# Layer 1 of a two-layer graph network: the running weighted sum, the projections, bias and gate accumulated in PSUM

## The chip, the core and the metric

The kernel runs on one core of one Trainium2 chip. The metric is the device time of one execution in microseconds (us), the median of several runs. TensorE (PE in the profile), VectorE (DVE), ScalarE (ACT) and GpSimd (POOL) each take their instructions in program order and wait for each other through semaphores; the SyncE queue (SP) issues plain DMAs, and GpSimd issues all indirect DMAs (gathers and scatters).

## What is computed

A graph of 3327 nodes with 512 features each and an adjacency matrix `adj` with few ones per row (at most 128 rows of nodes have many). Layer 0 is a four-head graph attention; its result is added to `x` and normalised. This `x` goes into layer 1, which the change is about. Cut to what matters, with `adj` as both of its adjacencies:

```
type_sum = adj @ x
attn_a = sigmoid(concat(type_sum, x) @ Wa.T + ba)        # one number per node
attn_b = sigmoid(concat(type_sum, x) @ Wb.T + bb)
h = x @ W_sa
scores = s_left[:, None] + s_right[None, :]              # two dot products of h with a_sa
e = where(adj != 0, exp(-leaky_relu(scores, 0.01)), 0)
attn = e / (sum(e, axis=1) + 1e-5)
x_a = attn @ h
x_b = adj @ (x @ W_gcnb) + b_gcnb
x = layernorm(x + sigmoid(attn_a * x_a + attn_b * x_b))
```

## The kernel before

Everything is float32. The nodes are sorted by degree and cut into 26 tiles of 128 nodes, in two groups of 12 and 14. `CAPS[j]` says how many neighbours tile j needs at most (14 down to 4); a neighbour is a slot, and a slot of a tile is one gather of 128 rows of 520 floats (266 KB) by GpSimd (`indirect`, L615) into one of 42 slots of a ring in SBUF. The first tile of each group (`T0`) has one slot more, the "stair", for the few nodes with more neighbours than `CAPS`. Over layer 1 this makes 228 gathers: 226 slots and 2 stairs.

Layer 1 uses linearity: instead of summing rows of h and of `x @ W_gcnb`, it sums rows of x, weighted and plain, and projects the two sums. For one tile j:

- `own_score`, `weights_a`, `weights_b` (L1019 to L1065): VectorE and ScalarE make the weights `e[:, s]` of the slots, already multiplied by the gate `attn_a`, from columns that travel with the rows; `gates[j][:, 1:2]` is the gate `attn_b`. VectorE's L1032 is the first that reads a tile's gathered rows, L1039 is ScalarE's exp, L1062 the last scaling of the weights.
- `scaled_first` (L1067): ScalarE starts the weighted sum `sw`, an SBUF tile, with the node's own row (L1070). For a `T0` tile it also scales the stair and TensorE spreads it (`stair_sum`, L1075).
- `weighted` (L1077), in two parts: one VectorE instruction per slot adds row times weight onto `sw` (L1085, a scalar_tensor_tensor over 128x512).
- `plain_sum` (L1089): TensorE adds the rows up in PSUM, transposed already, four instructions a row (L1098).
- `turn`, `to_sbuf`, `project` (L1103 to L1118): TensorE transposes `sw` (L1107), ScalarE copies both sums from PSUM into SBUF (L1112; half 1 the plain, half 0 the weighted one), TensorE multiplies each with its weight matrix into PSUM tiles `po0` (one buffer) and `po1` (two buffers). A float32 instruction of the program runs as two rows of the trace there: the four steps of a `project` are eight rows "po L1118".
- L1147 to L1149: VectorE adds the bias to `po1` (L1147), multiplies by the gate and adds `po0` (L1148), ScalarE takes the tanh in SBUF (L1149). Later VectorE adds it to the residual (L1171), takes the statistics (L692), and every few tiles the normalisation runs (L701 to L708 on VectorE, L1161 on ScalarE) and GpSimd scatters the rows out (L146).

The order is written out by hand, as a software pipeline over 26 + 3 steps. In step i tile `j` = order[i] is summed, `j1` = order[i+1] gets its weights, `jp` = order[i-1] is projected, `jpp` = order[i-2] is finished. Within a step the order per engine is: TensorE `turn(jp)`, `plain_sum(j)`, `project(jp, 1)`, `project(jp, 0)`, then the small products for `j1` if it is a `T0` tile; VectorE `weighted(j, 0)`, bias and gate of `jpp`, `weights_a(j1)`, `weighted(j, 1)`, residual of `jpp`, `weights_b(j1)`, statistics; ScalarE the plain copy of `jp`, the weighted copy of `jp`, tanh of `jpp`, exp and gate of `j1`, normalisation, `scaled_first(j1)`. GpSimd issues gathers as soon as the ring has free slots, and the scatters of finished rows only when no gather is left.

Of the kernel before, what the change touches and what calls it, by code (L numbers as in the profile page):

```python
# [8 lines left out]
F32 = mybir.dt.float32  # L9
AF = mybir.ActivationFunctionType  # L10
ALU = mybir.AluOpType
# [3 lines left out]
P = 128  # L15
# [63 lines left out]
def sparse_pass(  # L79
# [39 lines left out]
    nc = tc.nc  # L119
    N, F = out.shape  # L120
    NP = x.shape[0]
    H, FO = a_self.shape
# [61 lines left out]
    def row1(j):  # L184
        g, i = place(j)
        return x1[g][:, i, :]
# [827 lines left out]
        order += long[:1] + short[:1]  # L1014
        short, long = short[1:], long[1:]
    order += last
    ew, gates, sums, plain, proj, zs, stair_sum = {}, {}, {}, {}, {}, {}, {}

    def own_score(j):  # L1019
        ew[j] = m1.tile([P, S + 1], F32, tag="e", name=f"e{j}", bufs=3)  # L1020
# [2 lines left out]
    def weights_a(j):  # L1023

        c = slots(j)
        e = ew[j]
        gate = gates[j] = m1.tile([P, 12], F32, tag="gate", name=f"gate{j}", bufs=5)
        if j in T0:
            small = ps1.tile([P, B * H], F32, tag="small", name=f"to_nodes1_{j}")
            cols = to_nodes(m1, small, f"l1_{j}", stair[j][:, F : F + 3])  # L1030
        for s0, n, g, _ in got[j]:
            nc.vector.tensor_scalar(e[:, s0 : s0 + n], g[:, :n, F], row1(j)[:, F + 3 : F + 4], None, ALU.add)  # L1032
# [12 lines left out]
        if j in T0:  # L1045
            nc.vector.tensor_reduce(
                gate[:, 4 + 2 * parts : 6 + 2 * parts], cols[:, :, 1:3].rearrange("p b i -> p i b"), AX.X, ALU.add
            )
            parts += 1
        nc.vector.tensor_add(gate[:, 0:2], gate[:, 4:6], row1(j)[:, F + 4 : F + 6])  # L1050
        for i in range(1, parts):
            nc.vector.tensor_add(gate[:, 0:2], gate[:, 0:2], gate[:, 4 + 2 * i : 6 + 2 * i])

        nc.scalar.activation(gate[:, 0:2], gate[:, 0:2], AF.Tanh, scale=0.5)

    def weights_b(j):
# [5 lines left out]
        nc.vector.tensor_scalar(e[:, :c], e[:, :c], gate[:, 2:3], gate[:, 0:1], ALU.mult, ALU.mult)  # L1062
        if j in T0:
            small = ps1.tile([P, B * H], F32, tag="small", name=f"to_rows1_{j}")
            ws2[j] = to_rows(m1, small, f"l1_{j}", e[:, C0 + 1 :].rearrange("p (b o) -> p b o", o=1))  # L1065

    def scaled_first(j):  # L1067

        sw = sums[j] = m1.tile([P, F], F32, tag="sw", name=f"sw{j}")
        nc.scalar.activation(sw, row1(j)[:, 0:F], AF.Copy, scale=ew[j][:, 0:1])  # L1070
        if j in T0:
            scaled = m1.tile([P, F], F32, tag="scaled", name=f"scaled{j}", bufs=1)
            nc.scalar.activation(scaled, stair[j][:, 0:F], AF.Copy, scale=ws2[j])
            stair_sum[j] = ps1.tile([P, F], F32, tag="stair", name=f"stair_sum{j}")
            nc.tensor.matmul(stair_sum[j], to_node, scaled, start=True, stop=True)  # L1075

    def weighted(j, part):  # L1077

        e, sw = ew[j], sums[j]
        cut = 2 + (CAPS[j] * 5 + 7) // 8  # L1080
        for s0, n, g, _ in got[j]:
            for i in range(n):
                s = s0 + i
                if (s < cut) == (part == 0):
                    nc.vector.scalar_tensor_tensor(sw, g[:, i, 0:F], e[:, s : s + 1], sw, ALU.mult, ALU.add)  # L1085
        if part == 1 and j in T0:
            nc.vector.tensor_add(sw, stair_sum[j], sw)

    def plain_sum(j):  # L1089

# [20 lines left out]
        sT = zs[j, half] = m1.tile([P, KT, P], F32, tag=f"sT{half}", name=f"sT{half}_{j}")  # L1111
        nc.scalar.copy(sT, (turned, plain)[half][j])  # L1112

    def project(j, half):
        sT, wt = zs[j, half], (wsa, wg)[half]
        po = proj[j, half] = ps1.tile([P, F], F32, tag=f"po{half}", name=f"po{half}_{j}", bufs=1 + half)
        for k in range(KT):
            nc.tensor.matmul(po, sT[:, k, :], wt[:, k, :], start=(k == 0), stop=(k == KT - 1))  # L1118

    ends = {3, 7, 11, 15, 19, 22, 24, 25}  # L1120
    norm = Norm(m1, "n1", ends)
# [9 lines left out]
    for i in range(NT + 3):  # L1131
        j, j1, jp, jpp = at_(i), at_(i + 1), at_(i - 1), at_(i - 2)
        if i > 0 and jp is not None:
            free(jp)
        gather()
        if j1 is not None:
            own_score(j1)
        if jp is not None:
            to_sbuf(jp, 1)
            turn(jp)  # L1140
            to_sbuf(jp, 0)
        if j is not None:
            plain_sum(j)
            weighted(j, 0)
        if jpp is not None:
            za = zs[jpp] = m1.tile([P, F], F32, tag="za", name=f"za{jpp}", bufs=3)
            nc.vector.tensor_add(za, bias_g, proj[jpp, 1])  # L1147
            nc.vector.scalar_tensor_tensor(za, za, gates[jpp][:, 1:2], proj[jpp, 0], ALU.mult, ALU.add)  # L1148
            nc.scalar.activation(za, za, AF.Tanh, scale=0.5)  # L1149
        if jp is not None:  # L1150
            project(jp, 1)
            project(jp, 0)
        if j1 is not None:
            weights_a(j1)
        if j is not None:
            weighted(j, 1)
        if ready:
            k0, scale, shift = ready
            for k in range(k0, i - 2):
                z = row1(order[k])[:, 0:F]  # L1160
                nc.scalar.activation(  # L1161
                    z, z, AF.Identity, scale=scale[:, k - k0 : k - k0 + 1], bias=shift[:, k - k0 : k - k0 + 1]
                )
                outs.append((own(order[k]), z))
            ready = None
        while outs and not waiting:
            scatter("out", out, *outs.pop(0), N - 1)
        if jpp is not None:
            za = zs[jpp]
            zs[jpp] = row1(jpp)[:, 0:F]  # L1170
            nc.vector.scalar_tensor_tensor(zs[jpp], za, 0.5, zs[jpp], ALU.mult, ALU.add)  # L1171
        if j1 is not None:
            weights_b(j1)
            scaled_first(j1)
        if jpp is not None:
            ready = norm.add(i - 2, zs[jpp])

# [451 lines left out]
```

## Time and profile before

| | us |
|---|---|
| time before, median of 3 runs (1057.76 to 1071.53) | 1068.92 |
| profiled execution, its own time | 897.77 |
| its span, from the first to the last instruction | 895.8 |
| TensorE busy / VectorE busy / GpSimd busy / ScalarE busy | 745.3 / 693.3 / 595.2 / 272.0 |
| first and last issue of the 228 gathers of layer 1 | 530.94 / 842.26 |
| end of TensorE's last instruction of layer 1 | 879.8 |
| mean granted TensorE clock | 0.908 |

The span is one execution recorded by the profiler; 1.97 us lie around it. The median of the runs is 171.15 us above the profiled execution's own time. The profile page doesn't say where these are. Times of instructions below are microseconds from the start of the span. A group line gives the count, the busy time, the mean duration of one in ns, and the idle time of the engine before it with what ended it. A line of the timeline gives the start, the length, the engine and the count of the merged instructions.

### The profile page before, as it was taken

What the parts mean: (1) busy time and instruction counts of PE and PEld (TensorE: products, weight loads), DVE (VectorE), ACT (ScalarE), POOL (GpSimd) and SP (SyncE); (2) the same over time, 40 slices, a digit from 0 to 9 for tenths busy, and PEclk for the clock granted to TensorE, in tenths of its full rate; (3) what the DMA queues carried; (4) which work ended last, traced back from release to release, by engine and by line L of the source; (5) the groups of instructions that cost most, each with busy time, mean ns of one, the idle gap of its engine ahead of it and who ended that gap; (6) DMA issues with size and microseconds to landing.
All of it is one profiled execution on the core that took longest, in us unless ns stands there. A gap on an engine that the chain in (4) does not pass through costs nothing. (4 is left out here: it accounts for less than half of the span.)

```text
span 895.8 us, 11378 instructions
## 1 busy us (share of the span) xinstructions
PE 745.3 (83%) x3118; PEld 457.4 (51%) x3118; DVE 693.3 (77%) x2032; ACT 272.0 (30%) x794; POOL 595.2 (66%) x641
## 2 busy tenths in 40 slices
PE   4698997416799978799999957987997999999992
PEld 3477775103445534344444435654764666666551
DVE  4288787896678858769898845957996999998973
ACT  0122221002335525444646512212222222232231
POOL 6711133566577777777777747777777777777772
PEclk9799999556899989889999967999898999999997
DMA  8989999999777878789777637677767777777641
GB/s 330 369 340 403 366 377 345 380 387 399 267 225 227 276 234 263 231 278 329 219 234 228 222 115 203 188 199 201 187 184 196 192 196 195 203 193 199 195 187 74
DMA packets 73352, 224.74 MB, mean 251 GB/s; under 512 B 12736, under 2 KB 16784, under 8 KB 72384
## 3 DMA queue, kind: packets, MB, share of 16 engines
q0 software_dynamic: 46368, 153.69, 56.9%
q1 hardware_dynamic: 24256, 68.13, 19.9%
q10 hardware_dynamic: 2656, 2.10, 0.7%
q8 instruction: 27, 0.44, 0.2%
q14 instruction: 45, 0.37, 0.1%
HBM read 203.02 MB, written 31.51 MB: 262 GB/s over the span
## 5 line engine op out<-in xcount | busy, mean ns | idle before, releaser
L615 POOL DMA_INDIRECT ring<-table,srt x464 | 475.7, 1025 | 162.1 <-issue 56.2
L803 PE MATMUL acc<-ring,ident 128*128 128x512 f32 x504 | 239.4, 619 | 18.9 <-DVE ring L802 12.9
L1085 DVE SCALAR_TENSOR_TENSOR sw<-ring,e,sw 128x512 f32<-128x512 f32 x226 | 169.8, 751 | 10.7 <-ACT sw L1070 4.2
L803 PEld LDWEIGHTS acc<-ring,ident 128*128 128x128 f32 x504 | 94.4, 196 | 130.3 <-issue 74.3
L371 PE MATMUL pf<-w,xc 128*128 128x260 f32 x416 | 102.9, 410 | 13.1 <-DVE w L311 13.1
L1098 PE MATMUL acc<-ident,ring 128*128 128x128 f32 x904 | 108.6, 280 | 6.2 <-DMA ring<-table,srt 6.1
L797 DVE TENSOR_TENSOR ring<-ring,w 128x512 f32<-128x512 f32 x176 | 111.8, 693 | 0.5
L1098 PEld LDWEIGHTS acc<-ident,ring 128*128 128x128 f32 x904 | 103.6, 145 | 8.1 <-DMA ring<-table,srt 8.1
L1118 PE MATMUL po<-wsa,sT 128*128 128x512 f32 x208 | 95.4, 602 | 4.6 <-DVE za L1148 2.3
L371 PEld LDWEIGHTS pf<-w,xc 128*128 128x128 f32 x416 | 84.1, 205 | 29.3 <-DVE w L311 13.8
L1118 PE MATMUL po<-wg,sT 128*128 128x512 f32 x208 | 93.6, 593 | 0.0
L795 ACT ACTIVATE ring<-ring,w 128x128 f32<-128x128 f32 x304 | 91.5, 390 | 0.0
L383 POOL DMA_DIRECT2D table<-row x26 | 14.2, 549 | 85.2 <-ACT st L380 82.6
L1118 PEld LDWEIGHTS po<-wsa,sT 128*128 128x128 f32 x208 | 39.7, 193 | 56.6 <-issue 56.1
L1118 PEld LDWEIGHTS po<-wg,sT 128*128 128x128 f32 x208 | 37.5, 190 | 37.3 <-issue 37.3
L1149 ACT ACTIVATE za<-za 128x512 f32<-128x512 f32 x26 | 16.4, 630 | 127.7 <-DVE za L1148 127.7
L402 PE MATMUL pc<-at,pow 128*32 128x512 bf16 (+1 forms) x182 | 23.3, 413 | 35.3 <-DMA at<-in_adjB 25.4
L762 ACT ACTIVATE w<-w 128x40 f32<-128x40 f32 (+10 forms) x26 | 6.2, 237 | 127.5 <-DVE w L761 127.5
L375 ACT COPY row<-pf 128x512 f32<-128x512 f32 x26 | 15.2, 586 | 95.4 <-PE pf L371 49.7
L834 PEld LDWEIGHTS pcol<-v,xt 128*128 128x128 f32 x208 | 28.7, 201 | 14.5 <-issue 12.1
L828 ACT COPY xt<-x1t 128x512 f32<-128x512 f32 x26 | 15.2, 584 | 62.9 <-PE x1t L822 62.9
L402 PEld LDWEIGHTS <-pow 128*32 128x32 bf16 x182 | 7.3, 97 | 47.9 <-issue 44.8
(252 smaller groups left out, 918.4 us busy)
## 6 DMA issues: line engine op xcount, KB each, us to landing
at<-in_adjB SPq DMA_DIRECT2D x78, 512.0 KB, 11.5
ring<-table,srt POOLq DMA_INDIRECT x464, 3.9
table<-row POOLq DMA_DIRECT2D x26, 260.0 KB, 6.1
xc<-in_xB SPq DMA_DIRECT2D x6, 1024.0 KB, 8.4
own<-in_xo SPq DMA_DIRECT2D x1, 3640.0 KB, 46.5
own<-table SPq DMA_DIRECT2D x1, 3640.0 KB, 55.2
at<-in_adjL SPq DMA_DIRECT2D x13, 256.0 KB, 9.9
table<-in_xo SPq DMA_DIRECT2D x1, 3120.0 KB, 27.2
```

Source lines behind the costliest of these rows:

```text
L371: nc.tensor.matmul(pf[:, hh, :HC], xc[:, k, o : o + P], w0[:, k, hh, :], start=(k == 0), stop=(k == KT - 1))
L375: nc.scalar.copy(row[:, 0:F].rearrange("p (h o) -> p h o", h=2), pf[:, :, 0 : F // 2])
L402: nc.tensor.matmul(pc[32 * c : 32 * c + 32, : nt * P], pow2[:, s, :], loaded[i, m], start=(s == 0), stop=(m + 1 not in ms or s == 3),)
L615: return nc.gpsimd.indirect_dma_start(out=out_, out_offset=None, in_=table, in_offset=bass.IndirectOffsetOnAxis(ap=ap, axis=0)).ins
L795: nc.scalar.activation(gv[:, h, :], gv[:, h, :], AF.Copy, scale=w[:, s, h : h + 1])
L797: nc.vector.tensor_tensor(gv, gv, w[:, s, :].rearrange("p (h o) -> p h o", o=1).to_broadcast([P, H, FO]), ALU.mult)
L803: nc.tensor.matmul(acc, ident, row, start=(lean and s == 0), stop=(s == CAPS[j] and j not in T0))
L834: nc.tensor.matmul(pcol, xt1[:, k, :], v1[:, k, :], start=(k == 0), stop=(k == KT - 1))
L1085: nc.vector.scalar_tensor_tensor(sw, g[:, i, 0:F], e[:, s : s + 1], sw, ALU.mult, ALU.add)
L1098: nc.tensor.matmul(pl[:, k, :], row[:, k * P : (k + 1) * P], to_node if steps else ident, start=(i + k == 0), stop=(i == len(rows) - 1 and ...
L1118: nc.tensor.matmul(po, sT[:, k, :], wt[:, k, :], start=(k == 0), stop=(k == KT - 1))
L1149: nc.scalar.activation(za, za, AF.Tanh, scale=0.5)
```

## The change

The weighted sum `so_far` lives in PSUM now: ScalarE writes its first term there, VectorE reads and writes it there, and only the last slot's instruction writes the result into an SBUF tile `sw`[...]. The projections have no PSUM tiles of their own any more: `gated` is seeded with the bias by a ScalarE copy, TensorE adds the plain projection onto it, ScalarE multiplies by the gate and writes the product as the seed of `za0` or `za1` (in turns), TensorE adds the weighted projection onto that, and ScalarE takes the tanh from there. VectorE's two instructions per tile for bias and gate are gone. The plain copy (`to_sbuf(j, 1)`) moves from the start of the next step to the end of the tile's own step, behind `scaled_first(j1)`, together with the bias seed; `project(jp, 1)` moves to the start of TensorE's step, ahead of `turn(jp)`; tanh of `jpp` moves to the start of ScalarE's step. `stair_sum` shares the PSUM tile of the small products. At the start of layer 1 three products with the identity write the bias into the three PSUM tiles once.

```diff
     def scaled_first(j):
-        sw = sums[j] = m1.tile([P, F], F32, tag="sw", name=f"sw{j}")
-        nc.scalar.activation(sw, row1(j)[:, 0:F], AF.Copy, scale=ew[j][:, 0:1])
+        so_far[j] = ps1.tile([P, F], F32, tag="so_far", name=f"so_far{j}")
+        nc.scalar.activation(so_far[j], row1(j)[:, 0:F], AF.Copy, scale=ew[j][:, 0:1])
...
-            stair_sum[j] = ps1.tile([P, F], F32, tag="stair", name=f"stair_sum{j}")
+            stair_sum[j] = ps1.tile([P, F], F32, tag="small", name=f"stair_sum{j}")
...
     def weighted(j, part):
-        e, sw = ew[j], sums[j]
-        cut = 2 + (CAPS[j] * 5 + 7) // 8
+        e, sw = ew[j], so_far[j]
+        if part == 1:
+            sums[j] = m1.tile([P, F], F32, tag="sw", name=f"sw{j}")
+        cut = min(2 + (CAPS[j] * 5 + 7) // 8, CAPS[j])
...
-                    nc.vector.scalar_tensor_tensor(sw, g[:, i, 0:F], e[:, s : s + 1], sw, ALU.mult, ALU.add)
+                    to = sums[j] if s == CAPS[j] else sw
+                    nc.vector.scalar_tensor_tensor(to, g[:, i, 0:F], e[:, s : s + 1], sw, ALU.mult, ALU.add)
         if part == 1 and j in T0:
-            nc.vector.tensor_add(sw, stair_sum[j], sw)
+            nc.vector.tensor_add(sums[j], stair_sum[j], sums[j])
...
-    def project(j, half):
-        sT, wt = zs[j, half], (wsa, wg)[half]
-        po = proj[j, half] = ps1.tile([P, F], F32, tag=f"po{half}", name=f"po{half}_{j}", bufs=1 + half)
+    gated = ps1.tile([P, F], F32, name="gated")
+    zas = [ps1.tile([P, F], F32, name=f"za{n}") for n in range(2)]
+    for to in (gated, *zas):
+        nc.tensor.matmul(to, ident, bias_g, start=True, stop=True)
+
+    def project(n, j, half):
+        sT, wt = zs[j, half], (wsa, wg)[half]
+        po = gated if half else zas[n % 2]
         for k in range(KT):
-            nc.tensor.matmul(po, sT[:, k, :], wt[:, k, :], start=(k == 0), stop=(k == KT - 1))
+            nc.tensor.matmul(
+                po, sT[:, k, :], wt[:, k, :], start=False, stop=(k == KT - 1), skip_group_check=True
+            )
+        if half:
+            nc.scalar.activation(zas[n % 2], gated, AF.Copy, scale=gates[j][:, 1:2])
+
+    def plain_done(j):
+        nc.scalar.copy(gated, bias_g)
+        to_sbuf(j, 1)
...
         if j1 is not None:
             own_score(j1)
+        if jpp is not None:
+            za = zs[jpp] = m1.tile([P, F], F32, tag="za", name=f"za{jpp}", bufs=3)
+            nc.scalar.activation(za, zas[i % 2], AF.Tanh, scale=0.5)
         if jp is not None:
-            to_sbuf(jp, 1)
+            project(i - 1, jp, 1)
             turn(jp)
             to_sbuf(jp, 0)
         if j is not None:
             plain_sum(j)
             weighted(j, 0)
-        if jpp is not None:
-            za = zs[jpp] = m1.tile([P, F], F32, tag="za", name=f"za{jpp}", bufs=3)
-            nc.vector.tensor_add(za, bias_g, proj[jpp, 1])
-            nc.vector.scalar_tensor_tensor(za, za, gates[jpp][:, 1:2], proj[jpp, 0], ALU.mult, ALU.add)
-            nc.scalar.activation(za, za, AF.Tanh, scale=0.5)
         if jp is not None:
-            project(jp, 1)
-            project(jp, 0)
+            project(i - 1, jp, 0)
...
         if j1 is not None:
             weights_b(j1)
             scaled_first(j1)
+        if j is not None:
+            plain_done(j)
```

More of the change, by code (lines that the diff above doesn't have):

```diff
@@ L1016, in sparse_pass @@
     order += last
-    ew, gates, sums, plain, proj, zs, stair_sum = {}, {}, {}, {}, {}, {}, {}
+    ew, gates, sums, plain, proj, zs, stair_sum, so_far = {}, {}, {}, {}, {}, {}, {}, {}
     def own_score(j):
@@ L1028, in weights_a @@
         if j in T0:
-            small = ps1.tile([P, B * H], F32, tag="small", name=f"to_nodes1_{j}")
+            small = ps1.tile([P, F], F32, tag="small", name=f"to_nodes1_{j}")
             cols = to_nodes(m1, small, f"l1_{j}", stair[j][:, F : F + 3])
@@ L1063, in weights_b @@
         if j in T0:
-            small = ps1.tile([P, B * H], F32, tag="small", name=f"to_rows1_{j}")
+            small = ps1.tile([P, F], F32, tag="small", name=f"to_rows1_{j}")
             ws2[j] = to_rows(m1, small, f"l1_{j}", e[:, C0 + 1 :].rearrange("p (b o) -> p b o", o=1))
     def scaled_first(j):
-        sw = sums[j] = m1.tile([P, F], F32, tag="sw", name=f"sw{j}")
-        nc.scalar.activation(sw, row1(j)[:, 0:F], AF.Copy, scale=ew[j][:, 0:1])
+        so_far[j] = ps1.tile([P, F], F32, tag="so_far", name=f"so_far{j}")
+        nc.scalar.activation(so_far[j], row1(j)[:, 0:F], AF.Copy, scale=ew[j][:, 0:1])
         if j in T0:
```

## The prediction

> **What bounds the kernel now.** I read the windows first, to see which engine is full in layer 1 (from 530 on).
>
> ```profile
> 560.00:600.00 40.00, 35.79 (x173) 23.89 (x172) 28.53 (x63) 9.05 (x25) 31.16 (x30) 0.96 0.70 195
> 640.00:680.00 40.00, 40.00 (x193) 25.66 (x192) 33.68 (x76) 8.10 (x21) 31.37 (x29) 1.00 0.69 187
> 680.00:720.00 40.00, 33.76 (x173) 23.62 (x173) 35.06 (x78) 11.50 (x28) 31.16 (x30) 0.91 0.72 197
> 720.00:760.00 40.00, 40.00 (x218) 27.66 (x217) 37.30 (x90) 11.58 (x29) 31.16 (x30) 1.00 0.71 194
> 760.00:800.00 40.00, 40.00 (x199) 25.85 (x198) 37.25 (x87) 11.54 (x32) 31.17 (x30) 1.00 0.72 196
> ```
>
> Columns: length, then busy us and count of PE, weight loads, DVE, ACT, POOL, then the granted clock. TensorE is full, or nearly. VectorE is at 93% late and 71% early. GpSimd looks less busy (78%), but its count hardly moves: about 30 instructions per 40 us whatever the others do. The timeline tells why: it never stops.
>
> ```profile
> 721.74 0.75 DVE L1148 SCALAR_TENSOR_TENSOR za<-za,gate,po 128x512 f32<-128x512 f32 x1
> 722.62 0.95 POOL L615 DMA_INDIRECT ring<-table,srt  x1 [0.31 <-PE acc L1098]
> 727.80 0.95 POOL L615 DMA_INDIRECT ring<-table,srt  x1 [0.30 <-DMA ring<-table,srt]
> 729.96 4.69 DVE L1085 SCALAR_TENSOR_TENSOR sw<-ring,e,sw 128x512 f32<-128x512 f32 x6
> 730.30 1.23 POOL L615 DMA_INDIRECT ring<-table,srt  x1 [0.30 <-DMA ring<-table,srt]
> 731.83 1.27 POOL L615 DMA_INDIRECT ring<-table,srt  x1 [0.30 <-DMA ring<-table,srt]
> 733.41 1.27 POOL L615 DMA_INDIRECT ring<-table,srt  x1 [0.30 <-PE acc L1098]
> ```
>
> Before every gather lie the same 0.30 us: GpSimd issues gathers back to back, from 530.94 to 842.26, and no free slot is waited for. So the gathers are a stream with its own pace, 311.3/227 = 1.371 us each. And a gather takes 0.946 us, or up to 1.27 us while VectorE runs its weighted sum (L1085).
>
> Where TensorE idles, it idles for that stream. Its timeline:
>
> ```profile
> 594.49 1.09 PE L1107 MATMUL pt<-ident,sw 128*128 128x128 f32 x4 [4.21 <-DVE sw L1085]
> 626.72 0.57 PE L680 MATMUL to_rows<-e,to_row 128*128 128x10 f32 x2 [3.51 <-DVE e L1062]
> 686.71 0.57 PE L680 MATMUL to_rows<-e,to_row 128*128 128x10 f32 x2 [4.12 <-DVE e L1062]
> 688.49 2.08 PE L1075 MATMUL stair_sum<-scaled,to_node 128*128 128x512 f32 x2 [1.21 <-ACT scaled L1073]
> 836.02 5.37 PE L1118 MATMUL po<-wsa,sT 128*128 128x512 f32 x8 [1.94 <-DVE e L1032]
> ```
>
> VectorE is named, but VectorE waited itself: before 594 for tile 13's gathers (landed 592.7, exp at 593.4), before 627 and 687 for the two T0 tiles (last gathers issued at 618.1 and 677.4). From 690.4 to 879.8 TensorE has work all the time but for 1.94 us. So there are two bounds: the gather stream until 690, TensorE after.
>
> **The change, part by part.**
>
> *VectorE loses work.* Per tile L1147 and L1148 go:
>
> ```profile
> L1085 DVE SCALAR_TENSOR_TENSOR sw<-ring,e,sw 128x512 f32<-128x512 f32 x226 | 169.8, 751 | 10.7 <-ACT sw L1070 4.2 <-ACT e L1021 0.3
> L1148 DVE SCALAR_TENSOR_TENSOR za<-za,gate,po 128x512 f32<-128x512 f32 x26 | 19.4, 747 | 5.9 <-PE po L1118 3.5
> L1147 DVE TENSOR_TENSOR za<-bias_g,po 128x512 f32<-128x512 f32 x26 | 17.6, 679 | 0.0
> L1149 ACT ACTIVATE za<-za 128x512 f32<-128x512 f32 x26 | 16.4, 630 | 127.7 <-DVE za L1148 127.7
> ```
>
> That is 19.4 + 17.6 = 37.0 us, 1.43 per tile. It isn't the bound at any of the idle places, so by itself this is worth about nothing.
>
> *The sum in PSUM, VectorE's own price.* The 226 L1085 now read one operand from PSUM, and 200 of them write there. For reading, the row L1148 is the same operation with the same pointer and one operand in PSUM: 747 against 751 ns, no difference. [...] I take the row. No row shows VectorE writing PSUM. [...] I take 0. [...]
>
> *What it does to the gathers* is the part that pays. I set each gather's length against the VectorE instruction running 0.1 us after its start. L1085, both operands in SBUF: mean 1.18 us over 116 gathers; where it is still running then, the length is 0.82 us plus the time at which that instruction ends (end at 0.351: 1.172; at 0.449: 1.268). L1148 and L885, one operand each in PSUM, and L1147 too: 0.945 to 0.947, none longer (9, 12 and 12 gathers). So a gather waits at one point of its course for a VectorE instruction with two SBUF operands, and not for one with an operand in PSUM. The change turns all 226 into the second kind; only L1171 stays (11 gathers lie under it, by 0.19 us: 2 us in all). The new pace is 0.946 + 0.304 + 2/228 = 1.26 us, so gather n is issued (n - 1) x 0.111 us earlier: by its pace from 530.94, the 65th (first T0 tile) at 611.5 for 618.1, the 107th (second T0 tile) at 664.5 for 677.4, the last at 817 for 842.3. [...] by this trace it is 25 us at the stream's end. [...]
>
> *ScalarE* gets two more 128x512 per tile: the bias seed (as the copies L1112, 0.58 us, to the 0.72 of L1070) and the gated seed (the same bounds; a pointer as in L1070: 0.72). 1.3 us per tile on an engine at 11.5 of 40 us, hidden by TensorE's step of 11 us and more. If that cover goes, tanh and exp come later by as much.
>
> *TensorE* has the same work: per step 6.87 (16 rows po) + 0.44 (turn) + 0.437 per row of the plain sum; three products more at the start (about 4 us, under the wait for the first gathers). What changes is when a step may begin. Before: when the weighted sum of jp is done. After: when ScalarE has done the plain copy, which is queued behind `scaled_first(j1)`: 0.72 + 0.58 + 0.58 plus hops = 2.0 us after L1070 starts, that is some 3.7 us later against VectorE than now (L1171 0.69, `weights_b` 0.9). Behind the waiting product on TensorE stand turn, plain sum and all projections, and ScalarE's seed and exp wait for them. Before, TensorE began its step 1.5 to 4 us after L1070 from tile 22 to tile 2 (717.9 against 714.0; 754.2 against 752.7), and at 789 to 826 level with it. There VectorE just keeps pace: 12.3 us a step (839.6 + 11.3 - 703.4 over 12). It needs 12.3 - 1.43 = 10.9 then, TensorE 11.9 without its idle time, so after two or three steps the copy is there before TensorE is.
>
> *The sum.* Start: the first projecting step begins at 549.0 + 2.0 = 551.0 instead of 546.4; the 4.6 us are lost until the idle 4.21 us before 594.5, which swallow them. First T0 tile: all follows its gathers, 6.6 us earlier; step 7 starts at about 623.7 for 630.7. Steps 7 to 10 (46 plain rows): 4 x 7.3 + 46 x 0.437 = 49.3, TensorE is through at 673.0. The second T0 tile lets it go on where its gathers let it, 690.4 - 12.9 = 677.5, and 673.0 is before that. From there TensorE is the bound: 189.4 us as now, less the 1.94 us of idle time and the 1.8 us of slow restart behind it (5.37 for 3.60): the end is at 863.2 for 879.8, -16.6. Tail: L1148 goes from the path (-0.75), the seed's wait is bare once (+0.3). Total -17.0: the span 895.8 becomes 878.8, the profiled execution 897.8 becomes 880.8. GpSimd's 23 scatters after the last gather (1.3 each) end at 848, before TensorE. The median lies 171.2 us above the profiled execution; I carry that over as it is: 1068.9 - 17.0 = 1052. If the whole were stretched in proportion (1.19), it would be -20.
>
> **Rivals.**
> 1. The stream binds more in the timed runs than in the profile (what fills the 171 us isn't shown): all 25 us of it show, stretched by 1.19 to -30: 1039. For: GpSimd never pauses. Against: TensorE is full after 690.
> 2. The gathers don't get faster[...]: TensorE and the stream bind as now, -3 to +1: 1066 to 1070. For: no row has VectorE writing PSUM. Against: L1148 and L885 at 0.946.
> 3. Slower: the chain of sums through PSUM sets the pace, each waiting for the one before's write. VectorE has 1.0 us a step of room (11.9 - 10.9), so from 0.115 us more per slot, 0.87 us for an L1085, it decides, and each further 0.1 us costs 0.1 x 8.7 x 26 = 23 us. At 1.05 us: +41 - 17 = +24: 1093. For: the new start of a step hangs on VectorE's last instruction. [...]
>
> **How the numbers follow.** The case above 0.60, rival 1 0.10, rival 2 0.18, rival 3 0.12. About 2% (21.4 us) is what a measurement of this kernel tells from no change. The likeliest case's own range is -10 to -27 us (1042 to 1059); 0.25 of its 0.60 lie beyond -21.4, with rival 1 that is 0.35 faster; 0.35 + 0.18 = 0.53 within; 0.12 slower. The range runs from rival 1 (1038) past rival 2 and the scatter of the runs before (1074); rival 3 is left out.
>
> **What would show it.** Gathers of layer 1 at 0.95 to 0.97 us mean (now 1.067), the last one issued near 817; L1085's successor at 0.75; TensorE's waits before the second T0 tile ending near 677; TensorE's end near 863. Wrong if the gathers keep 1.07, if the sums take over 0.87, or if TensorE waits for the plain copy in most steps.

## The result, and the profile after

| | us |
|---|---|
| before, median of 4 runs (1057.76 to 1071.53) | 1066.88 |
| after, median of 4 runs (1091.94 to 1112.08) | 1096.9 |
| ratio after to before | 1.032, 95% interval 1.0229 to 1.041 |
| profiled execution after: own time, span | 1092.19, 1090.2 |
| first and last issue of layer 1's gathers | 616.4 / 992.9 |
| end of TensorE's last instruction of layer 1 | 1075.4 |

The change costs about 3%. (Ratios and intervals, here and below, are taken from each kernel's fast runs alone, those within 1.5% of its fastest, so they are not the quotients of the medians of all runs.) The profiled execution after is a typical one of its runs; that of before, 897.77 us, was not. The reason came out of the experiments and has to be told first. Each variant was timed beside the kernel before on one chip, and the chips are of two kinds. On one kind the unchanged kernel before takes 1067 to 1079 us (medians of each set of runs), on the other 896 to 898; none of the five chips on record was seen as both, and two were used twice. The chips of the first measurement are not on record; by its time the page of before is of the second kind, the times beside it and the page after are of the first. Below, "prompt chip" is the second kind and "late chip" the first, by what their traces differ in.

What the prediction said of single instructions came true. Groups of the kernel after (line, engine, operation, count, then busy us and mean ns of one, then idle time before them and what ended it):

```profile
L1088 DVE SCALAR_TENSOR_TENSOR so_far<-ring,e,so_far 128x512 f32<-128x512 f32 x200 | 151.0, 755 | 18.7 <-ACT x1a L1176 4.0 <-issue 3.1 <-ACT so_far L1070 3.1
L1088 DVE SCALAR_TENSOR_TENSOR sw<-ring,e,so_far 128x512 f32<-128x512 f32 x26 | 19.4, 745 | 1.7
L1131 ACT ACTIVATE za<-gated,gate 128x512 f32<-128x512 f32 x26 | 17.2, 662 | 95.0 <-PE gated L1127 63.8 <-PE acc L1101 14.2 <-PE pt L1110 7.3
L1135 ACT COPY gated<-bias_g 128x512 f32<-128x512 f32 x26 | 14.8, 571 | 0.0
```

The sum that reads and writes PSUM takes 755 ns for 751. But while gathers run, no engine is full in layer 1 any more. The windows of after (columns as before: PE, weight loads, DVE, ACT, POOL, clock, DMA share, GB/s):

```profile
660.00:700.00 40.00, 14.96 (x52) 7.99 (x52) 7.58 (x21) 5.21 (x13) 21.74 (x23) 0.61 0.56 153
860.00:900.00 40.00, 26.86 (x126) 17.37 (x127) 22.85 (x61) 8.54 (x22) 22.77 (x25) 0.86 0.59 167
900.00:940.00 40.00, 36.23 (x180) 23.52 (x179) 25.07 (x53) 14.26 (x34) 22.69 (x24) 0.96 0.56 155
940.00:980.00 40.00, 36.97 (x190) 24.15 (x189) 32.05 (x77) 14.27 (x35) 25.39 (x27) 1.00 0.64 177
```

GpSimd has 23 to 27 instructions per 40 us where before's page had 30, TensorE is idle for up to 25 of 40 us, and VectorE for more. TensorE's part of it in layer 1, from the waits of after (us in total, times, longest):

```profile
PE gated L1127 <- issue: 42.6, 8, 10.4
PE gated L1127 <- ACT sT L1115: 36.0, 2, 25.0
PE acc L1101 <- issue: 15.4, 13, 2.4
PE za L1127 <- issue: 9.9, 5, 2.6
```

In ten of 26 steps the first product of a step (`gated`) waits, 78.6 us in all, for ScalarE's plain copy L1115: each of the ten starts 0.05 us after the end of a copy, also where the view names only "issue". The first two, at the start of layer 1, make 35.4 us of it. The copy is queued right after ScalarE's bias seed, so the timelines of TensorE and ScalarE show what the copy waits for. After, on a late chip:

```profile
882.87 4.97 PE L1101 MATMUL acc<-ident,ring 128*128 128x128 f32 x44
887.67 3.60 PE L1127 MATMUL za<-wsa,sT 128*128 128x512 f32 x8
898.61 5.78 PE L1127 MATMUL gated<-wg,sT 128*128 128x512 f32 x8 [7.34 <-issue]
...
886.77 0.57 ACT L1135 COPY gated<-bias_g 128x512 f32<-128x512 f32 x1
897.97 0.58 ACT L1115 COPY sT<-acc 128x512 f32<-128x512 f32 x1 [10.64 <-remote]
```

The same kernel on a prompt chip (run a2 below):

```profile
705.93 3.66 PE L1101 MATMUL acc<-ident,ring 128*128 128x128 f32 x32
709.42 3.60 PE L1127 MATMUL za<-wsa,sT 128*128 128x512 f32 x8
712.86 3.60 PE L1127 MATMUL gated<-wg,sT 128*128 128x512 f32 x8
...
708.19 0.57 ACT L1135 COPY gated<-bias_g 128x512 f32<-128x512 f32 x1
709.62 0.58 ACT L1115 COPY sT<-acc 128x512 f32<-128x512 f32 x1 [0.87 <-PE acc L1101]
```

On the prompt chip the plain sum ends at 705.93 + 3.66 = 709.59 and the copy starts at 709.62. On the late chip the plain sum ends at 887.84, ScalarE is idle, and the copy starts at 897.97, 10.1 us later; TensorE has 3.6 us of other work and then idles 7.34 us. The view calls the releaser "remote", but the trace's record of TensorE's own semaphore has an update at 897.95, so it is TensorE that the copy waited for. The granted clock is no explanation of this wait: it was full until 896, when the copy was 8 us late already.

```profile
870.00:896.00 26.00, 21.27 (x119) 14.61 (x117) 19.11 (x49) 6.60 (x17) 16.41 (x18) 1.00 0.60 171
896.00:903.00 7.00, 4.39 (x6) 1.91 (x7) 2.70 (x8) 1.27 (x3) 1.54 (x2) 0.51 0.43 121
```

So on late chips the other engines learn late that TensorE has finished. I counted it in the traces: of ScalarE's and VectorE's instructions in layer 1 that sat idle for a product, a turn or a plain sum (over 0.3 us), how many started more than 1 us after its recorded end (the n-th copy set against the n-th sum, and so on). The last column counts updates of TensorE's semaphore in layer 1 that follow the one before within 0.2 us:

| trace | kernel | late | updates close together |
|---|---|---|---|
| page of before | before | 0 of 20 | 2 of 277 |
| e4b_order, a2 | order alone, after (prompt chips) | 0 of 29, 0 of 61 | 2 of 255, 2 of 279 |
| b0 | before (late chip) | 32 of 55, median 6.5 us | 54 of 254 |
| after | after (late chip) | 22 of 59, median 5.8 us | 45 of 256 |
| e4d_order | order alone (late chip) | 24 of 47, median 4.8 us | 31 of 234 |

On prompt chips the delay in these is 0.04 us nearly every time, and the updates of TensorE's semaphore stand close behind recorded ends (275 of the 277 on the page of before by 0.013 to 0.015 us; 0.01 to 0.02 in a2). So on late chips either TensorE itself ends later than recorded, or its updates come late. Updates do come late: a plain sum gives one per row, every 0.437 us on the page of before, while those of the last column stand less than 0.2 us apart (31 of the 45 in after: 0.06 us), less than a row takes. I take it that the work they report had been done before. One such burst in b0, by those who waited:

```profile
934.01 0.59 ACT L1112 COPY sT<-acc 128x512 f32<-128x512 f32 x1 [11.32 <-PE acc L1098]
937.01 0.59 ACT L1112 COPY sT<-pt 128x512 f32<-128x512 f32 x1 [2.41 <-PE acc L1098]
...
936.86 0.69 DVE L1147 TENSOR_TENSOR za<-bias_g,po 128x512 f32<-128x512 f32 x1 [9.53 <-PE acc L1098]
```

VectorE, idle for 9.53 us, sees `po1` done at 936.86; ScalarE sees the turn done at 937.01. By the records the two ended at 924.28 and 929.99, with eight rows of `po0` between them; they became visible 0.15 us apart. On the page of before eight rows of `po` take 3.4 us at full clock (0.429 from start to start), so that work had been done before. But TensorE itself is held up as well. In b0, from 670 to 712, it starts one short instruction every 0.7 to 3.5 us, and the view shows nothing that it waits for:

```profile
695.50 0.37 PE L1098 MATMUL acc<-ident,ring 128*128 128x128 f32 x1 [2.42 <-issue]
698.30 0.37 PE L1098 MATMUL acc<-ident,ring 128*128 128x128 f32 x1 [2.44 <-issue]
701.10 0.37 PE L1098 MATMUL acc<-ident,ring 128*128 128x128 f32 x1 [2.42 <-issue]
```

On the page of before 24 of these take 2.78 us, 0.11 us from start to start. The granted clock is 0.50 in this stretch of b0; where it is 0.50 on the page of before, these start 0.21 us apart (median of 56), not 2.8. Both kernels do this on late chips: after starts single products at 654.43, 657.22 and 660.02. What holds TensorE up is not shown.

### The profile page after: what moved, and what is told of

Read it like the earlier page. It is cut to its first block, busy times and chain, and to the rows that moved or that the text cites. A ratio compares the mean times of both kernels' runs of the same rounds, so it can differ in the third digit from the quotient of the medians.

```text
span 1090.2 us, 11334 instructions
## 1 busy us (share of the span) xinstructions
PE 782.0 (72%) x3124; PEld 464.2 (43%) x3124; DVE 659.4 (60%) x1980; ACT 299.9 (28%) x846; POOL 570.6 (52%) x641
## 5 line engine op out<-in xcount | busy, mean ns | idle before, releaser
L615 POOL DMA_INDIRECT ring<-table,srt x464 | 455.7, 982 | 304.6 <-issue 96.2
L803 PE MATMUL acc<-ring,ident 128*128 128x512 f32 x504 | 253.1, 649 | 63.0 <-DVE ring L802 31.0
L803 PEld LDWEIGHTS acc<-ring,ident 128*128 128x128 f32 x504 | 98.8, 206 | 182.0 <-issue 93.0
L1127 PE MATMUL gated<-wg,sT 128*128 128x512 f32 x208 | 112.2, 689 | 78.6 <-issue 42.6
L1088 DVE SCALAR_TENSOR_TENSOR so_far<-ring,e,so_far 128x512 f32<-128x512 f32 x200 | 151.0, 755 | 18.7 <-ACT x1a L1176 4.0
L1127 PEld LDWEIGHTS gated<-wg,sT 128*128 128x128 f32 x208 | 45.7, 225 | 144.5 <-issue 103.2
L1127 PE MATMUL za<-wsa,sT 128*128 128x512 f32 x208 | 97.3, 608 | 10.8 <-issue 9.9
L1127 PEld LDWEIGHTS za<-wsa,sT 128*128 128x128 f32 x208 | 38.4, 195 | 50.0 <-issue 48.9
L1115 ACT COPY sT<-acc 128x512 f32<-128x512 f32 x26 | 15.1, 583 | 119.0 <-remote 97.4
L1131 ACT ACTIVATE za<-gated,gate 128x512 f32<-128x512 f32 x26 | 17.2, 662 | 95.0 <-PE gated L1127 63.8
L1037 DVE SCALAR_TENSOR_TENSOR e<-e 128x9 f32<-128x9 f32 (+10 forms) x26 | 4.5, 173 | 57.8 <-ACT e L1021 55.5
```

The costliest lines, as they stand in the source:

```text
L615: return nc.gpsimd.indirect_dma_start(out=out_, out_offset=None, in_=table, in_offset=bass.IndirectOffsetOnAxis(ap=ap, axis=0)).ins
L803: nc.tensor.matmul(acc, ident, row, start=(lean and s == 0), stop=(s == CAPS[j] and j not in T0))
L1088: nc.vector.scalar_tensor_tensor(to, g[:, i, 0:F], e[:, s : s + 1], sw, ALU.mult, ALU.add)
L1127: nc.tensor.matmul(po, sT[:, k, :], wt[:, k, :], start=False, stop=(k == KT - 1), skip_group_check=True)
L1131: nc.scalar.activation(zas[n % 2], gated, AF.Copy, scale=gates[j][:, 1:2])
```

## The experiments

Each kernel is timed against the kernel before on the same chip.

**The two halves of the change, late chip.** `e1_sum` has only the running sum in PSUM; `e2_gate` only the projections, bias and gate in PSUM, with the new order; `b0` and `a0` are before and after unchanged, run for their traces and times. Theory A: the new start of a step, behind the plain copy, costs; theory B: the sum in PSUM costs.

```diff
e1_sum, against before:
-        sw = sums[j] = m1.tile([P, F], F32, tag="sw", name=f"sw{j}")
+        so_far[j] = ps1.tile([P, F], F32, tag="so_far", name=f"so_far{j}")
...
-                    nc.vector.scalar_tensor_tensor(sw, g[:, i, 0:F], e[:, s : s + 1], sw, ALU.mult, ALU.add)
+                    to = sums[j] if s == CAPS[j] else sw
+                    nc.vector.scalar_tensor_tensor(to, g[:, i, 0:F], e[:, s : s + 1], sw, ALU.mult, ALU.add)
e2_gate, against after: these lines taken back, all else kept
```

> The kernel before, unchanged, for a trace of an execution that takes what the timed runs take. The profile page of before showed 898 us, its timed runs 1067; the changed kernel's profile shows 1092, like its timed runs, with layer 1 starting at 616 instead of 531. Theory A (the page of before shows an execution with quick gathers that timed runs don't have): the trace takes about 1067 us, its layer 1 starts near 616 too, and GpSimd pauses between gathers there, as in the changed kernel. Theory B (the changed kernel itself brings the pauses): about 1067 us, but layer 1 starts near 531 and the rest is after the end of layer 1 or in front.

> The changed kernel once more, on the chip and beside the runs that the two halves are compared with: +30 us against before (1.03) by either theory, with the same pauses of GpSimd as in its first trace if they belong to every execution.

> Only the running weighted sum is in PSUM; bias, gate, projections and their order stay as before. Theory A (what costs is the new start of a TensorE step, behind ScalarE's plain copy): 0 to -25 us against before, as the gathers under the sum get to 0.946 us and nothing is added. Theory B (the sum in PSUM costs, through its reads and writes or by what the faster gathers do): +20 to +40 us, as the whole change.

> Only projections, bias and gate are summed up in PSUM, with the new order of a step; the weighted sum stays in SBUF. Theory A: +25 to +50 us against before (the change without its quick gathers). Theory B: 0 to -10 us.

Measured: e1_sum 1074.08 for 1077.97, ratio 0.9997 (0.9924 to 1.007); e2_gate 1087.82, 1.0091 (1.0003 to 1.0178); a0 1107.04, 1.0215 (1.0135 to 1.0295). b0, the same program as before, came out at 1069.67 and 0.991 (0.9823 to 0.9998), so 0.9% alone tells little here. Its traced execution was its longest, 1090.83. Theory B, with its 20 to 40 us, falls: the sum in PSUM costs nothing that shows (0.7% at most). A has the sign, but the order's half shows 10 us where A said 25 to 50. Three places of the cause were still possible: the copy's place in ScalarE's queue (A1), the late completion itself (A2), the seeds (B, in a new sense).

**Four variants, prompt chip.** These shared a chip on which before takes 897.1 us.

```diff
e3_early, against after:
+        if j is not None:
+            plain_done(j)
...
             weights_b(j1)
             scaled_first(j1)
-        if j is not None:
-            plain_done(j)
e4_order, against before:
-            to_sbuf(jp, 1)
+            project(jp, 1)
             turn(jp)
...
-            project(jp, 1)
             project(jp, 0)
...
             scaled_first(j1)
+        if j is not None:
+            to_sbuf(j, 1)
e5_oldorder, against after (plain_done moved as well, tanh ahead of weights_a):
-            project(i - 1, jp, 1)
+            plain_done(jp)
             turn(jp)
...
-            project(i - 1, jp, 0)
+            project(i - 1, jp, 1)
...
             weights_a(j1)
+        if jp is not None:
+            seed(i - 1, jp)
+            project(i - 1, jp, 0)
e6_deeper, against e5_oldorder (tanh, residual and statistics a step later, one more buffer for the weighted copy):
+            seed(i - 2, jpp)
...
             plain_done(jp)
...
             project(i - 1, jp, 1)
...
-            seed(i - 1, jp)
-            project(i - 1, jp, 0)
+            project(i - 2, jpp, 0)
```

> The changed kernel with one move: bias seed and plain copy of tile j are queued on ScalarE ahead of weights_b(j1) and scaled_first(j1), no longer behind them. Three theories. A1 (the step's first product waits because its copy is queued behind scaled_first, that is behind VectorE): most of the loss comes back, ratio to before 1.00 to 1.01, and TensorE's idle time ahead of the first gated product falls from about 80 us to under 40. A2 (it waits because the plain sum's completion itself reaches ScalarE late, up to 13 us after the recorded end, and only project(jp, 0), 3.6 us, lies between): nothing changes, ratio 1.015 to 1.035, idle time still 65 to 95. B (the seeds make TensorE and ScalarE wait for each other in turns, wherever the copy stands): as A2.

> The kernel before with the order alone: plain copy at the end of the tile's own step, project(jp, 1) first on TensorE, ahead of turn(jp); sum, bias and gate stay on VectorE and in SBUF, no seeds. A1 and A2 (the order is the cost, without any of the PSUM sums): slower than before, ratio 1.01 to 1.03, with 50 us or more of TensorE idle time ahead of the first product of a step. B (the seeds are the cost): ratio 0.995 to 1.005 and under 25 us there.

> The changed kernel with all sums in PSUM, but TensorE's order of before (turn, plain sum, project(jp, 1), project(jp, 0)), bias and plain copy at the start of the next step, tanh of jpp ahead of weights_a(j1), the gate's seed behind exp. A1 and A2: the cover of the copy is back; what is left is the seed's round trip ahead of project(jp, 0), 26 times 1 to 2 us when completions come on time: ratio 1.00 to 1.015. B: the round trip between two products is bare and every late completion goes into it: ratio 1.025 or more, idle time ahead of the first za product over 80 us.

> All sums in PSUM with TensorE's order of before, and project(jpp, 0) of the tile before last in the place of project(jp, 0), so that copy and seed both have a whole step of cover; each tile is finished one step later. A1 and A2: no product waits for a copy or a seed for long, VectorE has 37 us less and gathers are shorter: ratio 0.985 to 1.00. B: the seeds still alternate, but with a step of slack: 1.00 to 1.01. If ratio over 1.015, neither order nor cover is the cause, and the sums in PSUM themselves are.

Repeats, meant for a late chip, came to other prompt chips:

> The kernel before with the order alone, as e4_order, on whatever chip this is. Where before takes about 1070 us and completions come late: A2 (late completions under an order with little cover, no PSUM needed) says 1.01 to 1.03 of before and 50 us or more of TensorE idle time ahead of the first product of a step; B (the seeds are what is exposed) says 0.995 to 1.005 and under 25 us. Where before takes 897 us: 1.004 again.

> The kernel before with the order alone, hoped for on a chip where before takes about 1070 us and completions come late. A2 (late completions under an order with little cover; no sum in PSUM needed): 1.01 to 1.03 of before and 50 us or more of TensorE idle time ahead of the first product of a step. B (the seeds are what is exposed): 0.995 to 1.005 and under 25 us. Where before takes 897 us: 1.004 a third time.

> All sums in PSUM, TensorE's order of before, the seed between the two products of a tile, as e5_oldorder. Where completions come late: A2 says that the copy's cover is back but the seed's round trip has none, so late completions go into it: 1.01 to 1.03, with the idle time (60 us or more) now ahead of the za product and not ahead of the gated one; B the same. Only if it is 1.00 or below is the round trip harmless. Where before takes 897 us: 1.0075 again.

> All sums in PSUM, TensorE's order of before, and the weighted projection one step later, as e6_deeper. Where completions come late: A2 says that copy and seed have a step of cover, no long waits ahead of a product, ratio 0.98 to 1.00; B says 1.00 to 1.015, over 50 us of idle time ahead of the products that follow a copy or a seed. Where before takes 897 us: 0.9875 again.

> All sums in PSUM, TensorE's order of before, the weighted projection one step later. Where before takes about 1070 us: A2 says 0.98 to 1.00 and no long waits ahead of a product; B says 1.00 to 1.015 and over 50 us of idle time ahead of the products that follow a copy or a seed. Where before takes 897 us: 0.988 to 0.992 again.

> All sums in PSUM, TensorE's order of before, the weighted projection one step later. On a chip where before takes about 1070 us, A2, now shown by e4d_order, says 0.98 to 1.00 of before, no long waits ahead of a product; if it is 1.015 or more, cover for copy and seed is not enough and the loss has a part that the order doesn't explain. Where before takes 897 us: 0.988 to 0.992.

> The changed kernel, unchanged, beside these three. Where before takes about 1070 us: 1.02 to 1.03. Where before takes 897 us and completions come on time: A2 says 0.985 to 1.003, A1 and B say 1.01 or more.

Measured, all on prompt chips:

| kernel | median us (before 896 to 898) | ratio, 95% interval |
|---|---|---|
| e3_early | 890.21 | 0.9924 (0.9893 to 0.9955) |
| e4_order, e4b, e4c | 899.87, 900.03, 900.99 | 1.0039, 1.0038, 1.0034 (each within 1.0015 to 1.006) |
| e5_oldorder, e5b | 904.85, 903.8 | 1.0075, 1.0073 (1.0047 to 1.0103) |
| e6_deeper, e6b, e6c, e6d | 885.43, 888.22, 888.17, 889.73 | 0.9875, 0.9918, 0.9901, 0.9909 (0.9838 to 0.9945) |
| a2 (after unchanged) | 888.4 | 0.9921 (0.9896 to 0.9947) |

The first expectations for e3 and e4 had been made for a chip on which after loses, so neither run decides between the theories. a2 does in part: a loss whatever the chip, 1.01 or more by A1 and B, is not there. With prompt completions after is faster than before by 0.8%, and the order alone costs 0.4%. On one chip a2 and e4b differ by 11.6 us: that is what the PSUM parts bring there. (e6b had been expected at 0.9875 again and came at 0.9918.) The waits of e5b, in layer 1, price the seed's round trip:

```profile
PE za L1127 <- ACT za L1133: 22.3, 26, 2.1
```

Standing bare between the two products of a tile it costs 0.75 us in 24 steps and 2.1 in the T0 steps. After and e6_deeper put work between; on one chip they took 888.40 and 888.22, so there the extra step of cover brought nothing that shows.

**After and the earlier copy, late chip.**

> The changed kernel, unchanged, once more. The kernel before took about 1070 us on the chip of the first measurements and 897 us on that of the runs e3 to e6, where every completion of TensorE reached the others 0.04 us after its recorded end. If this chip is like the second: theory A2 (the loss comes from late completions under an order that leaves them little cover) says that the change is no loss there, ratio 0.985 to 1.003; A1 and B (the order or the seeds cost whatever the chip) say 1.01 or more. If it is like the first: ratio 1.015 to 1.035 again.

> The changed kernel with bias seed and plain copy queued ahead of weights_b(j1) and scaled_first(j1), as e3_early, beside a1 on one chip. If before takes about 1070 us here: A1 says 1.00 to 1.01 of before, A2 and B within 0.01 of a1's ratio. If it takes about 897 us: 0.99 again, and the distance to a1 is what the place behind scaled_first costs where completions come on time: by A1 0.01 or more, by A2 under 0.008.

Measured: a1 1095.78 for 1071.56, ratio 1.0221 (0.9979 to 1.0463), an interval that reaches below 1; e3b_early 1096.75, with no interval (its four runs took 1082 to 1112). Both waits of TensorE are there in either, first a1, then e3b_early:

```profile
PE gated L1127 <- issue: 34.6, 6, 11.0
PE gated L1127 <- ACT sT L1115: 33.6, 2, 29.8
```

```profile
PE gated L1127 <- ACT sT L1115: 37.0, 2, 29.1
PE gated L1127 <- issue: 24.5, 7, 8.5
```

68.2 and 61.5 us, and the same median. A1 had said under 40 us and most of the loss back, A2 65 to 95 us. So taking the copy out from behind `scaled_first(j1)`, and so from behind VectorE, doesn't remove the waits; that it saves some microseconds is not excluded by runs that scatter by 30 us.

**The order alone, late chip.** The fourth run of this kernel is the first on a late chip, and the one that decides.

> The kernel before with the order alone, once more. On a chip where before takes about 1070 us, A2 says 1.01 to 1.03 of before and 50 us or more of TensorE idle time ahead of the first product of a step; B says 0.995 to 1.005 and under 25 us. Where before takes 897 us: 1.003 to 1.004.

Measured: 1096.9 for 1078.99, ratio 1.0263 (1.0084 to 1.0443). TensorE's waits in layer 1, first of e4d_order, then of b0 (before):

```profile
PE po L1118 <- issue: 73.5, 13, 32.7
PE to_rows L680 <- DVE e L1062: 16.0, 2, 12.7
PE acc L1098 <- issue: 11.6, 16, 1.9
```

```profile
PE acc L1098 <- issue: 52.0, 53, 3.1
PE pt L1107 <- issue: 10.0, 6, 5.6
PE to_rows L680 <- DVE e L1062: 7.6, 2, 4.3
...
PE po L1118 <- issue: 3.1, 8, 0.7
```

There is no sum, seed or gate in PSUM in this kernel, and it loses about as much as the whole change does (1.8% even if all seven runs of before beside it are taken). B, which had said 0.995 to 1.005, falls as the only cause. The order, A2's place for it, is enough for a loss. By the group lines of the two pages, e4d_order and then b0, most of the wait stands ahead of the plain product, which the new order puts first:

```profile
L1118 PE MATMUL po<-wg,sT 128*128 128x512 f32 x208 | 109.1, 674 | 68.1 <-issue 66.1
L1118 PE MATMUL po<-wg,sT 128*128 128x512 f32 x208 | 104.4, 644 | 2.7 <-issue 2.0
```

The late completions are in b0 too, but there the plain copy's product comes after turn and plain sum. TensorE's gaps of over 0.15 us in layer 1 come to 79 us in b0, and to 109 in e4d_order and 118 in after. Much of this is one long hold-up near the start of layer 1, which every late trace has. b0 spends it in the short stops shown above; e4d_order has these for a while and then stands for 32.7 us:

```profile
664.45 1.01 PE L1118 MATMUL po<-wsa,sT 128*128 128x512 f32 x1 [1.13 <-issue]
667.29 1.01 PE L1118 MATMUL po<-wsa,sT 128*128 128x512 f32 x1 [1.83 <-issue]
701.00 5.50 PE L1118 MATMUL po<-wg,sT 128*128 128x512 f32 x7 [32.70 <-issue]
```

So this stop is no measure of what the order costs. Cut at the start of the fourth turn, layer 1 took, in us:

| trace | first gather to fourth turn | from there to TensorE's end |
|---|---|---|
| page of before, a2 (prompt) | 48.4, 57.4 | 300.5, 284.6 |
| b0, e1_sum (late, order of before) | 95.8, 94.5 | 338.9, 342.7 |
| e4d_order, e2_gate (late, new order) | 99.2, 98.8 | 349.1, 347.7 |
| e3b_early (late, new order, earlier copy) | 98.8 | 342.6 |
| after, a0, a1 (late) | 96.5, 99.2, 99.2 | 362.5, 361.6, 355.8 |

These are single executions. In them the order costs 3 to 5 us at the start and 5 to 10 behind it, the whole change 1 to 5 and 13 to 24. So the timed runs show that the order loses, but its traces account for only part of the loss. The earlier copy's trace is 13 to 20 us shorter behind the fourth turn than the three of after, though its median is no better: whether the copy's place (A1) costs something on late chips stays open.

e6_deeper, the kernel that gives copy and seed a step of cover, was run four times and always on prompt chips. Whether cover takes the loss away on a late one was not measured, so A2's "little cover" is argued from the waits. No version is shown to beat both kernels on both kinds of chip.

## Why the prediction was wrong

It said 1052 us and the change gave 1096.9. Two of its steps failed and turned the result, one in the frame of the sum and one term inside; a third made the gain too large.

*The carry-over.* "The median lies 171.2 us above the profiled execution; I carry that over as it is." This is the step that turned the sign. The 171 us were taken as a constant beside the kernel; they lie inside it, as idle time and as slower work of TensorE. b0's span is 192.9 us longer than the page's, 107 of it up to the first gather of layer 1 (638.2 for 530.94) and 86 from there to the end (450.5 for 364.9); TensorE is busy for 802.3 us instead of 745.3, at a mean granted clock of 0.838 instead of 0.908. What they come to depends on the order of the work, as e4d_order's 1.0263 shows. A page whose own time is 16% below the median of the runs describes another regime, and "TensorE is full" and "GpSimd never pauses" were true of that regime alone: b0's TensorE idles 79 us in layer 1, and GpSimd waits 50 us there for slots that VectorE and TensorE free (26.4 and 23.6). Nor could the page show the delay: none of its waits has it.

*The cover of a step's start.* "so after two or three steps the copy is there before TensorE is." On the prompt chip this is right: a2's plain product waits for the copy once, 10.3 us in the first step, and not again. On the late chip it waits in ten of 26 steps of after, 78.6 us, and eight of them, 43.2 us, come later than the second step: the copy starts up to 14.6 us after the plain sum there, and 3.6 us of `project(jp, 0)` cover it. The prediction had named the waiting product and what is queued behind it, but measured the path through VectorE and `scaled_first`, without which e3b_early still waits 61.5 us, and put TensorE's own completion at nothing.

*The size, where the mechanism held.* On prompt chips the sum was to be -17.0 us and is -7.9 (896.26 to 888.4). By its terms, from the trace of a2: the gathers did what was forecast (mean 0.956 us for 0.95 to 0.97, last issue at 815.5 for 817). The first step starts at 549.7, 3.3 us later (forecast 4.6), and is made good by tile 13 as forecast. After the second T0 tile TensorE saves 4.0 us (forecast 3.7). What failed is "the second T0 tile lets it go on where its gathers let it": the step there starts 4.4 us earlier (686.0 for 690.4), not 12.9. On the page of before the prediction had read VectorE rightly, it did wait for gathers there:

```profile
681.94 0.19 DVE L668 TENSOR_TENSOR spread_l<-step_of,ring 128x30 f32<-128x30 f32 x1 [5.88 <-DMA ring<-table,ids]
```

But TensorE was through with its own queue only at 681.28, so earlier gathers could free no more than 0.9 us. The timeline of a2 at that place:

```profile
675.57 2.31 PE L1127 MATMUL za<-wsa,sT 128*128 128x512 f32 x5
677.71 0.30 PE L673 MATMUL to_nodes<-spread_l,to_node 128*128 128x30 f32 x2
678.05 0.23 DVE L1034 SCALAR_TENSOR_TENSOR e<-to_nodes,x1a,no_step 128x10 f32<-128x10 f32 x1 [8.94 <-PE to_nodes L673]
...
681.64 0.52 DVE L1062 TENSOR_SCALAR e<-e,gate 128x25 f32<-128x25 f32 x1
682.31 0.57 PE L680 MATMUL to_rows<-e,to_row 128*128 128x10 f32 x2 [4.30 <-DVE e L1062]
```

The gathers are there (VectorE reads them at 668.75), and VectorE waits 8.94 us for `to_nodes`, a small product queued on TensorE behind plain sum and projection. From its end at 678.0 to the step's start at 686.0 the weights make a round trip from TensorE through VectorE and ScalarE, with 4.3 us of idle time for TensorE, as 4.12 before. The sum had TensorE "through at 673.0" and put nothing behind it. It was through at 677.9: the first T0 tile, bound in the same way, let it go at 626.1 and not 623.7, and the four steps took 51.7 us, not 49.3. With the 8 us of round trip that makes the 8.5 us that are missing, less the 4.5 us that the forecast gave to the wait for gathers.

*The other points.* VectorE's price for PSUM is nil, as taken from the row L1148: L1088, with an operand in PSUM, takes 755 ns writing PSUM (200 of them) and 745 writing SBUF (26), for 751 of L1085 with both in SBUF. Gathers under the sum's instruction were to be no longer than 0.945 to 0.947: after, the 96 that have L1088 running 0.1 us after their start take 0.945 in the mean. On late chips shorter gathers gain nothing that shows (e1_sum, 0.9997): GpSimd waits for slots there, and in e1_sum's trace one is issued every 1.552 us for b0's 1.576, though they take 0.961 us in the mean for 1.057. ScalarE's two instructions cost 0.571 and 0.662 for 0.58 and 0.72; on the prompt chip they are hidden as said. Rival 3 named the place ("the new start of a step") and nearly the time, 1093, but by a price that does not exist: its 1.05 us per slot is 0.755. Its sum was nearly right by accident, and the forecast's range left it out. Rival 1 was the opposite of what happened, rival 2 is excluded by the gathers' lengths.

What stays open: what delays the completions, and holds up TensorE itself, on late chips, in layer 0 as well (ahead of the first gather, 60 of TensorE's 378 updates in after stand over 1 us behind the recorded end before them, and none of 450 on the page of before; its gaps of over 0.15 us come to 162 us there for 90). It goes along with gathers in flight: after the last gather was issued (992.9), in after, ScalarE's waits are back at 0.04 us from 1019 on, and TensorE is busy 40.00 of the 40 us from 1022. But prompt chips run the same gathers, and faster (one per 1.261 us in a2, per 1.659 in after), without it. It isn't shown either why e2_gate, which has the new order too, lost 0.9% and e4d_order 2.6%; their intervals overlap. And on the chip of e2_gate the whole change lost 2.15%, so that the seeds or the sum add something to the order's loss on late chips is not excluded.

## What to carry to other kernels

Before a page is used to forecast a median, set its own time against the median; if they are far apart, look for the difference in a trace of an execution that has it, and until then allow that waits between engines are longer by several us each (here 4.8 to 6.5 in the median of those that came late). A handoff from TensorE over another engine back to TensorE should have more work between than it needs on paper: here 3.6 us of cover were enough at 0.04 us of delay, and the order that has no more than that lost 2 to 3% where completions came up to 15 us late. And an idle time named after an engine is to be followed one step further than the engine that was waited for: behind the T0 tiles it led back to TensorE's own queue.

## What the runs showed of the hardware

- The same program takes 897 us on some chips and 1070 on others, with VectorE's, ScalarE's and GpSimd's instructions equally long on both (a2 and after: L1088 755 and 755 ns, L1131 662 and 662, gathers 956 and 951). TensorE's completions are seen 0.04 us after the recorded end on the one kind, and up to 15 us after it in ordinary steps on the other (35 to 51 us near the start of layer 1, in the three late traces counted above), in bursts; there TensorE also starts single instructions 0.7 to 3.5 us apart without a wait (b0, 670 to 712), and its mean granted clock is lower (0.838 to 0.853 in the traces, for 0.904 to 0.919).
- A gather issued by GpSimd is not stretched by a VectorE instruction that reads one operand from PSUM (0.945 us, 96 gathers of after), where one with both operands in SBUF stretches it to 1.18 in the mean (116 gathers of the page before): the pace of the stream fell from 1.371 to 1.261 us (a2: 529.4 to 815.5 for 228 gathers). The sum in PSUM alone does it (e1_sum: 0.948 for 92 gathers).
- A handoff from TensorE through one 128x512 ScalarE instruction back to TensorE costs 0.75 us when nothing covers it (e5b_oldorder, prompt chip, 24 of 26 tiles).
